# Macaron block (tree FFN, MLA attention, tree FFN): leaf-innermost w1 columns, w2 in 16 pieces, weight loads on ScalarE's queue, a table product on VectorE, and first rows of the next tree ahead

## The chip, the cores and the metric

The kernel runs on one core of a Trainium2 chip, in one launch, in fp32 (masks, positions and routing tables are bf16 where they are exact). The metric is the device time of that core in microseconds (us). The kernel before took 2531.09 us (median of 3 runs, 2529.74 to 2541.51). Engines are named as in the profile: PE is TensorE (PEld its weight loads), DVE is VectorE, ACT is ScalarE, POOL is GpSimd, SP is SyncE, which only issues DMAs. A "queue" is an engine's own list of instructions that issue DMAs: an instruction that waits there holds everything behind it on that engine.

## The reference

`x` is (4, 1024, 256), that is 4096 tokens of width 256. The block is a half-weighted FFN, an attention layer and a second half-weighted FFN with the same weights:

```python
x = x + 0.5 * ffn(layernorm(x))
x = x + attention(layernorm(x))
x = x + 0.5 * ffn(layernorm(x))

def tree(x, nw, nb, w1, b1, w2, b2, act):   # hard-routed, depth 8
    node = 0
    for _ in range(8):
        logit = x . nw[node] + nb[node]
        node = 2 * node + 1 + (logit > 0)
    leaf = node - 255                        # 256 leaves
    h = act(x @ w1[leaf] + b1[leaf])         # w1 (256, 256, 16)
    return h @ w2[leaf] + b2[leaf]           # w2 (256, 16, 256)

def ffn(x):
    xn = (x - mean) / sqrt(std + 1e-5)
    q, k, v = (tree(xn, ..., relu) for each of three trees)
    y = xn + softmax(q @ k.T / 16) @ v       # over all 1024 tokens of a row
    return y + tree(y, ..., gelu)            # the fourth tree, f
```

The attention layer has 16 heads of width 16, a latent of 128 for keys and values, rotary positions and a mask by pages of 64. The change does not touch it.

## The kernel before

**Stages.** Times are us from the span's start: FFN1 0 to 856 (routing to 117, tree q 117 to 223, tree k 232 to 328, tree v 333 to 441, softmax attention 444 to 770, tree f 770 to 856), attention layer 856 to 1690, FFN2 1690 to 2533 (routing to 1764, q 1764 to 1873, k 1874 to 1979, v 1983 to 2083, attention 2087 to 2410, then f and the output). The function `ffn` (L994) is called twice, for FFN1 with `first` set.

**Routing and sorting.** The 4096 tokens are 32 tiles of 128 in SBUF. `routes` (L421) takes the top five levels of trees q, k and v for four tiles at a time: `route` (L378) transposes the rows (L389), copies them (L392), multiplies by the nodes' weights (L397), compares (L405), and marks each token's block of 8 leaves (L409, L417); POOL adds up these marks (L419). The normalized rows also go to DRAM, `rows_x` (`keep_rows`, L372, on ACT's queue), 512 KB in each of 8 steps. Before each step `norms(k)` runs, which here also takes steps of `build` (below). `placement` (L530) then gives every token a slot, sorted by block, in blocks filled up to tiles of 128 slots: `low` computes ranks (matmuls L547, L548) and `high` the table `inv` of which token sits in which slot. In `high`, VectorE makes `tiles` (L589), ACT one half of `both` (L591), POOL the other half (L593), and PE multiplies (L596) into the table. Trees k and v are placed while the tree before them runs. `rest(3)` is the part of q's placement that remains once all tiles are routed; after its last step the first gather of tree q is issued (L806).

**A tree.** Each of q, k and v runs 48 tiles always, and up to 63 in the spare parts 48 to 53, 53 to 58, 58 to 63 under `tc.If` on the number of tiles used (`spare_leaves`, L772). In this data q and v take a spare part in one FFN or the other. `leaves` (L791) is a software pipeline over tiles: gather rows by `inv` (`load`, POOL's indirect DMA, L806, four tiles ahead, and past tile 47 too), transpose (`turn`, PE L817, ACT copy L819), multiply by the block's columns of w1, 128 columns for 8 leaves of 16 and 7 for the lower nodes (`hidden`, PE L835, L842), make the mask of the leaf that the token takes (DVE L851 to L858), mask the 128 columns (DVE L865), transpose and apply relu (`active`, PE L879, L880, ACT L888), multiply by w2 and b2 (`result`, PE L899, L900), copy out of PSUM (ACT L914, tile `og`, three buffers) and store (SP, L915). 

**Weights.** w1 arrives as (leaf, column of x, 16) in four raw parts of 1 MB (`load_part`, DMA L710, two buffers), is transposed by PE (L759) and copied to w1 by DVE (L762) and ACT (L764) in turn: `load_first` (L740) is a generator with 16 groups of four transposes and one copy, and issues raw parts 3 and 4 when 1 and 2 are used up. w2 is one 4 MB DMA to 128 partitions (`load_second`, L700), with partition (leaf, hidden column). b2 comes in three DMAs (L937), `sub` with the lower nodes in one (L744). `load_b1` (L717) makes b1 of all four trees in FFN1 by 48 small DMAs on SP (L724, L729) and POOL operations (L733 to L738). All these loads are issued from SP; ACT's queue carries `keep_rows`. While tree q runs, `with_steps` drains one step of k's placement per tile and one group of k's `load_first` per three tiles; the same with v during k. For tree q itself, `build` (the 16 groups of its `load_first`) is taken during `norms(k)` for k from 4 on, two groups each time, two more after `routes`, and the rest between the steps of `rest(3)`.

**Order.** Trees q and k and the routing are ordered by the Tile framework's scheduler; the attention and tree f are in program order (`in_order`). Completion of DMAs is counted on eight lanes shared by SP's and ACT's queues; an issue waits until its lane is free.

Of the kernel before, what the change touches and what calls it, by code (L numbers as in the profile page):

```python
# [77 lines left out]
def macaron_kernel(ctx: ExitStack, tc: tile.TileContext, a: dict, out: bass.AP):  # L78
# [107 lines left out]
    with tc.tile_pool(name="nodes", bufs=2) as np_, banks(0, 8):  # L186
        nwT = np_.tile([P, KC, len(FFFS), 2 * P], F32, name="nwT", bufs=1)
        nc.vector.memset(thr, 0.0)
        for f, nm in enumerate(FFFS):
            pt = [sm([P, 2 * P]) for _ in range(KC)]  # L190
            for lo in (0, NODES - P):
                nw = np_.tile([P, E], F32, name="nw", bufs=8)
                nc.sync.dma_start(nw, a[f"{nm}_nw"][lo : lo + P, :])
                for c in range(KC):
                    nc.tensor.transpose(
                        pt[c][:, lo : lo + P], nw[:, c * P : (c + 1) * P], ident
                    )
            lo = f % 3 * NBLK
            nc.scalar.dma_start(
                thr[lo : lo + NBLK - 1, f // 3 : f // 3 + 1],  # L200
                a[f"{nm}_nb"][: NBLK - 1].unsqueeze(1),
            )
            for c in range(KC):
                nc.vector.tensor_copy(nwT[:, c, f, :NODES], pt[c][:, :NODES])
            nc.scalar.dma_start(
                below[f].rearrange("p (c n) -> p c n", c=KC), nwT[:, :, f, NBLK - 1 : NODES]
            )
# [322 lines left out]
    def placement(pool, oh, acc, pieces, gblk, sel, own, inv, slot, ahead=False):  # L530
# [41 lines left out]
        def high(c, first, table):  # L572

            lo, hi = pieces[c]
            n, ts_ = hi - lo, slice(lo, hi)
            past, lane, in_lane = parts.pop(c)
            row = pool.tile([P, n, NBLK], F32, name="row", tag="row")
            nc.vector.tensor_tensor(row, oh[:, ts_, :], bc(first, 1, n), ALU.mult)
            at = pool.tile([P, n], F32, name="at", tag="at")
            nc.vector.tensor_reduce(at, row, AX.X, ALU.add)  # L580
            nc.vector.tensor_add(at, at, past)
            nc.vector.scalar_tensor_tensor(
                slot[:, ts_], at, float(P), lane, ALU.mult, ALU.add
            )
            yield
            tiles = pool.tile([P, n, GCOL], BF16, name="tiles", tag="tiles")
            at_b = pool.tile([P, n], BF16, name="at_b", tag="at_b")
            nc.vector.tensor_copy(at_b, at)
            nc.vector.tensor_tensor(tiles, bc(numbers, 1, n), bc(at_b, 2, GCOL), ALU.is_equal)  # L589
            both = pool.tile([P, n, 2, GCOL], BF16, name="both", tag="both", bufs=1 + ahead)  # L590
            nc.scalar.activation(both[:, :, 1], tiles, AF.Copy, scale=pid)  # L591
            yield
            nc.gpsimd.tensor_tensor(both[:, :, 0], tiles, bc(starts[:, ts_], 2, GCOL), ALU.mult)  # L593
            pi = sm([P, 2, GCOL])
            for i in range(n):
                nc.tensor.matmul(  # L596
                    pi, in_lane[:, i, :], both[:, i], start=(i == 0), stop=(i == n - 1)
                )
            yield
            if c:  # L600
                nc.vector.tensor_tensor(table, table, pi[:, 0], ALU.add)
            else:
                nc.vector.tensor_scalar_add(table, pi[:, 0], float(NTOK))
            nc.vector.tensor_tensor(table, table, pi[:, 1], ALU.add)
            yield
# [91 lines left out]
    def load_second(queue, pool, f):  # L697

        w2 = pool.tile([P, NBLK, E], F32, name=f"w2_{FFFS[f]}", tag="w2")
        dma = queue.dma_start(w2, a[f"{FFFS[f]}_w2"].rearrange("(b e) l d -> (e l) b d", e=EPB))  # L700
        if f != 3:
            tc.keep_in_program_order(dma)
        return w2
# [3 lines left out]
    def load_part(pool, f, hf, c, bufs=2):  # L707

        raw = pool.tile([P, P, LW], F32, name=f"raw_{FFFS[f]}{hf}{c}", tag="raw", bufs=bufs)
        nc.sync.dma_start(raw, a[f"{FFFS[f]}_w1"][hf * P : (hf + 1) * P, c * P : (c + 1) * P])  # L710
        return raw

    def load_raw(pool, f, bufs=2):

        return [load_part(pool, f, *p, bufs) for p in PART[:bufs]]

    def load_b1(pool, f):  # L717

        b1 = pool.tile([3 * NBLK, W1W], F32, name=f"b1_{FFFS[f]}", tag="b1", bufs=2)
        nb = a[f"{FFFS[f]}_nb"]  # L720
        nc.gpsimd.memset(b1[:, P + SUB :], 0.0)
        for k in range(3):
            at = slice(k * NBLK, (k + 1) * NBLK)
            nc.sync.dma_start(  # L724
                b1[at, :P], a[f"{FFFS[f]}_b1"].rearrange("(b e) l -> b (e l)", e=EPB)
            )
            for n in (1, 2, 4):
                lo = NBLK * n - 1
                nc.sync.dma_start(  # L729
                    b1[at, P + n - 1 : P + 2 * n - 1],  # L730
                    nb[lo : lo + NBLK * n].rearrange("(b j) -> b j", j=n),
                )
        nc.gpsimd.tensor_copy(b1p[f], b1)  # L733
# [6 lines left out]
    def load_first(pool, f, w1, raws, on_both=True, bufs=2):  # L740
# [3 lines left out]
        nc.sync.dma_start(sub, below[f].rearrange("p (c n) -> p c n", c=KC))  # L744
# [6 lines left out]
        for k, (hf, c) in enumerate(PART):  # L751
            raw = raws.pop(0)
            dst = w1[:, c, hf * nb_half : (hf + 1) * nb_half, :P].rearrange(
                "p b (e l) -> p l b e", l=LW
            )
            for l0 in range(0, LW, 4):
# [8 lines left out]
                if l0 + 4 == LW and k + 1 + len(raws) < len(PART):  # L765
                    raws.append(load_part(pool, f, *PART[k + 1 + len(raws)], bufs))
# [5 lines left out]
    def spare_leaves(*what):  # L772

        gblk = what[9]
# [9 lines left out]
        )  # L784
        with ExitStack() as es:
            for k in range(1, len(SPARE) - 1):
                es.enter_context(tc.If(used > SPARE[k], preferred_fallthrough_block=False))
                for _ in leaves(*what, k):
                    pass

    def leaves(pool, f, w1, w2, b2s, b1p, sel, own, inv, gblk, func, places, got, part=0):  # L791
# [5 lines left out]
        def load(g):  # L797
            width = E + (f == 3)
            if g < SPARE[1] + PRE:
                xg = pool.tile([P, width], F32, name="xg", tag="xg", bufs=PRE + 1 + 5 * (f // 3))  # L800
            else:
                xg = pool.tile([P, width], F32, name="xh", tag="xh", bufs=2 + 4 * (f // 3))
            if f == 3:
                nc.sync.dma_start(xg, xs_f[g * P : (g + 1) * P, :])
                return xg
            nc.gpsimd.indirect_dma_start(  # L806
                out=xg,
                out_offset=None,
                in_=rows_x,
                in_offset=bass.IndirectOffsetOnAxis(ap=inv[:, g : g + 1], axis=0),  # L810
            )
            return xg
# [8 lines left out]

        def hidden(g, xg, xT):
            if (g - lo) % REGS == 0:
                n = min(REGS, hi - g)
                _, vals = nc.values_load_multi_w_load_instructions(
                    gblk[:, g : g + n],
                    engines=[mybir.EngineType.PE],
                    min_val=0,
                    max_val=NBLK - 1,
                    skip_runtime_bounds_check_because="block numbers are limited by a minimum",  # L830
                )
                blk.update(zip(range(g, g + n), vals))
            ph = sm([P, P + SUB])
            for c in range(KC):
# [28 lines left out]
            )  # L863
            hm = pool.tile([P, P], F32, name="hm", tag="hm", bufs=3)
            nc.vector.tensor_tensor(  # L865
                hm.rearrange("p (e l) -> p e l", l=LW),
                ph[:, :P].rearrange("p (e l) -> p e l", l=LW),
                bc(mask[:, 0], 2, LW),
# [49 lines left out]
        end = hi if part else hi + PRE  # L918
        for g in range(lo - PRE, hi + 6):
            if g + PRE < end and g + PRE not in got:  # L920
# [73 lines left out]
    def ffn(first: bool, last: bool):  # L994
# [11 lines left out]
        with ExitStack() as es:  # L1006
# [25 lines left out]
            with ExitStack() as ws, banks(0, 8):  # L1032
# [5 lines left out]
                def tree(lp, f, *weights):  # L1038
                    return (
                        lp, f, *weights, b1p[f], sel[f], own[f], inv[f], gblk[f], AF.Relu, None, {}  # L1040
                    )

                with ExitStack() as hs, ExitStack() as rs:
# [11 lines left out]
                    with ExitStack() as rt:  # L1055
# [23 lines left out]
                        build = load_first(raw, 0, w1, load_raw(raw, 0))  # L1079
                        w2 = load_second(nc.sync, wp, 0)  # L1080
# [3 lines left out]
                        def norms(k):  # L1084
# [30 lines left out]
                            if k >= 4:  # L1115
                                drain(islice(build, 2))
# [3 lines left out]
                        drain(islice(build, 2))  # L1120
# [9 lines left out]
                    pp = stage(hs, "place", 1)  # L1130
                    for f in range(2):
                        what = tree(lp, f, w1, w2, b2s)
                        if first:
                            tc.keep_in_program_order(clear(nc.sync, osrt[f][SPARE[1] * P :]))
                        ahead = load_raw(raw, f + 1)
                        to = (wp, wb)[f == 0]
                        w1 = w1_of(to, f + 1)
                        w2 = load_second(nc.sync, to, f + 1)
                        b2s = load_b2(nc.sync, to, f + 1)
# [3 lines left out]
                            (3, load_first(raw, f + 1, w1, ahead)),  # L1143
                        )
                        spare_leaves(*what)
# [44 lines left out]
                what = tree(lp, 2, w1, w2, b2s)  # L1190
                with_steps(leaves(*what), (1, coming()))
                spare_leaves(*what)
# [10 lines left out]
            raws = load_raw(raw, 3)  # L1203
            with in_order(), qs, ExitStack() as ats, banks(2, 4):
                build = load_first(raw, 3, w1, raws)
# [152 lines left out]
            with banks(0, 8):  # L1358
                with in_order():
                    wp = stage(fs, "w2_f", 1, "right")  # L1360
                    w2 = load_second(nc.scalar, wp, 3)
# [13 lines left out]
                    )  # L1375
                    with_steps(leaves(*what), (1, reload()))
                spare_leaves(*what)
# [464 lines left out]
```

## Time and profile before

| what | us |
|---|---|
| median of 3 runs | 2531.09 (2529.74 to 2541.51) |
| the profiled execution's own time | 2534.66 |
| its span | 2532.9, mean granted TensorE clock 0.939 |
| PE busy | 2212.3 (87%) |
| DVE busy | 1450.0 (57%) |
| ACT busy | 1114.2 (44%) |
| POOL busy | 842.9 (33%) |

Shares of busy time are averages over stages with different limits. The profile page has the whole span in 40 slices; windows give busy time in a stretch; the timeline of one engine gives start, duration, engine, line, operation, output and inputs, count, and in square brackets the idle time of the engine just ahead of it with what ended it. A "q" behind an engine's name (SPq) marks its sequencer, which issues DMAs. A group of k instructions in a row is one line with the count at its end.

### The profile page before, as it was taken

The page shows a single profiled execution, that of the slowest core. Times are in us where ns is not written, and L with a number is a line of the kernel's source. Part 1 is how long each engine was busy: PE and PEld are TensorE (multiplying, and loading weights), DVE is VectorE, ACT ScalarE, POOL GpSimd, SP SyncE. Part 2 cuts the span into 40 slices and gives each one's busy share as a digit, 9 for nine tenths or more (in the row PEclk, how much of TensorE's full clock was granted, in tenths as well). Part 3 has the DMA queues.
Part 4 walks back from the last instruction along what each step waited for, and adds up shares of the span by engine and source line. Part 5 has one row for each costly group of instructions (what it writes and reads, how often), then busy time and mean ns, then how long its engine had stood idle before and what let it go on. Part 6 is the DMA issues. An engine that isn't in the chain of part 4 may idle for free. (4 is left out here: it accounts for less than half of the span.)

```text
span 2532.9 us, 43584 instructions
## 1 busy us (share of the span) xinstructions
PE 2212.3 (87%) x14203; PEld 1426.6 (56%) x14205; DVE 1450.0 (57%) x4720; ACT 1114.2 (44%) x2902; POOL 842.9 (33%) x1075
## 2 busy tenths in 40 slices
PE   4587988999978799999999999985979889999784
PEld 2376866666647644434344344334868766766473
DVE  6675844333446766666676677736857543334475
ACT  3354655233214225555555555552646552332142
POOL 5554565333144421101101100004545662431453
PEclk9798999999998889999999999987999899999897
DMA  9767675343065400000000000036675752430655
GB/s 320 247 196 214 173 217 154 98 126 109 22 189 150 127 1 1 1 1 1 1 18 1 1 18 12 8 136 222 174 206 165 214 158 94 134 106 23 186 158 166
DMA packets 208596, 288.03 MB, mean 114 GB/s; under 512 B 25449, under 2 KB 182522, under 8 KB 204256
## 3 DMA queue, kind: packets, MB, share of 16 engines
q1 hardware_dynamic: 133104, 156.89, 19.3%
q0 software_dynamic: 34304, 86.63, 13.0%
q10 hardware_dynamic: 40944, 41.43, 5.2%
q8 instruction: 132, 2.16, 0.4%
q14 instruction: 112, 0.92, 0.1%
HBM read 185.37 MB, written 104.32 MB: 114 GB/s over the span
## 5 line engine op out<-in xcount | busy, mean ns | idle before, releaser
L1592 DVE TENSOR_REDUCE mxh<-big 128x1 f32<-128x512 f32 (+3 forms) x768 | 392.9, 551 | 194.4 <-PE big L1584 192.5
L1628 ACT ACTIVATE pTh<-big 128x512 f32<-128x512 f32 (+3 forms) x768 | 341.3, 491 | 289.9 <-PE big L1584 266.2
L1584 PE MATMUL big<-kTh,qTh 32*128 32x512 f32 (+3 forms) x1536 | 402.2, 538 | 1.3 <-ACT kTh L1565 1.2
L1620 PE MATMUL big<-qTh,kTh 32*128 32x512 f32 (+3 forms) x1536 | 401.2, 537 | 2.1 <-ACT pTh L1628 1.8
L819 ACT COPY xgT<-sm 128x256 f32<-128x256 f32 x399 | 148.4, 373 | 288.4 <-PE sm L817 260.7
L990 PE MATMUL sm<-vb,pT 128*128 128x256 f32 x1024 | 237.2, 386 | 10.4 <-ACT pT L986 10.4
L962 PE MATMUL two<-kT,qT 128*128 128x512 f32 x512 | 236.2, 606 | 9.7 <-issue 8.2
L1620 PEld LDWEIGHTS big<-qTh,kTh 32*128 32x128 f32 x1536 | 143.4, 184 | 157.2 <-issue 126.8
L817 PE MATMUL sm<-ident,xg 128*128 128x128 f32 x792 | 162.0, 290 | 63.6 <-DMA xg<-rows_x,inv_v 17.5
L990 PEld LDWEIGHTS sm<-vb,pT 128*128 128x128 f32 x1024 | 193.1, 193 | 36.5 <-ACT pT L986 10.9
L970 DVE TENSOR_REDUCE mx<-two 128x1 f32<-128x1024 f32 x64 | 78.3, 1224 | 197.3 <-PE two L962 197.3
L851 DVE SCALAR_TENSOR_TENSOR went<-sm,sides 128x14 bf16<-128x14 f32 x399 | 67.5, 169 | 173.7 <-PE sm L842 165.6
L1639 PE MATMUL sm<-pTh,vpad 128*32 128x512 f32 (+3 forms) x1536 | 165.0, 501 | 0.0
L1584 PEld LDWEIGHTS big<-kTh,qTh 32*128 32x128 f32 x1536 | 146.2, 185 | 20.8 <-issue 14.5
L962 PEld LDWEIGHTS two<-kT,qT 128*128 128x128 f32 x512 | 94.6, 194 | 108.6 <-issue 105.0
L914 ACT COPY og<-sm 128x256 f32<-128x256 f32 x298 | 111.5, 375 | 93.3 <-DMA os_q<-og 24.6
L806 POOL DMA_INDIRECT xg<-rows_x,inv_k x104 | 104.6, 1006 | 107.0 <-PE sm L880 58.2
L806 POOL DMA_INDIRECT xg<-rows_x,inv_q x104 | 103.9, 999 | 90.6 <-PE sm L880 54.5
L817 PEld LDWEIGHTS sm<-ident,xg 128*128 128x128 f32 x792 | 86.5, 150 | 84.1 <-issue 44.5
L419 POOL TENSOR_TENSOR acc<-acc,oh 128x32 bf16<-128x32 bf16 (+1 forms) x128 | 41.3, 322 | 275.3 <-DVE oh L417 241.4
L905 POOL DMA_INDIRECT ytok<-og,tok x101 | 99.4, 984 | 82.5 <-DVE went L851 68.5
L992 DVE SCALAR_TENSOR_TENSOR xn<-sm,rs,xn 128x256 f32<-128x256 f32 x64 | 31.0, 485 | 162.2 <-PE sm L990 157.4
(364 smaller groups left out, 4697.8 us busy)
## 6 DMA issues: line engine op xcount, KB each, us to landing
xs_f<-zero ACTq DMA_DIRECT2D x14, 1028.0 KB
xg<-xs_f SPq DMA_DIRECT2D x104, 128.5 KB
os_q<-og SPq DMA_DIRECT2D x101, 128.0 KB
os_v<-og SPq DMA_DIRECT2D x101, 128.0 KB
os_k<-og SPq DMA_DIRECT2D x96, 128.0 KB
xn<-in_x SPq DMA_DIRECT2D x16, 512.0 KB
raw_q<-in_q_w SPq DMA_DIRECT2D x8, 1024.0 KB
w_q<-in_q_w SPq DMA_DIRECT2D x2, 4096.0 KB
```

The costliest lines, as they stand in the source:

```text
L806: nc.gpsimd.indirect_dma_start(out=xg, out_offset=None, in_=rows_x, in_offset=bass.IndirectOffsetOnAxis(ap=inv[:, g : g + 1], axis=0),)
L817: nc.tensor.transpose(pa[:, c, :], xg[:, c * P : (c + 1) * P], ident)
L819: nc.scalar.copy(xT, pa)
L905: nc.gpsimd.indirect_dma_start(out=places[g], out_offset=bass.IndirectOffsetOnAxis(ap=tok, axis=0), in_=og, in_offset=None, bounds_check=N ...
L914: nc.scalar.copy(og, po)
L962: nc.tensor.matmul(ps[:, n0 : n0 + 512], qT[:, c, i * P : (i + 1) * P], kT[:, c, n0 : n0 + 512], start=(c == 0), stop=(c == KC - 1),)
L990: nc.tensor.matmul(po, pT[:, j, :], vb[:, j, :], start=(j == 0), stop=(j == TPB - 1))
L1584: matmul = nc.tensor.matmul(ps[:, :n], qT[r : r + HPAD, hg, i * P : (i + 1) * P], kT[r : r + HPAD, hg, n0 : n0 + n], start=True, stop=True,)
L1592: nc.vector.tensor_reduce(maxima(b, hg)[:, i, c, u : u + 1], ps[:, :n], AX.X, ALU.max)
L1620: matmul = nc.tensor.matmul(ps[:, off:], kT[r : r + HPAD, hg, j * P : (j + 1) * P], qT[r : r + HPAD, hg, qb * QN + off : (qb + 1) * QN], s ...
L1628: nc.scalar.activation(pT[:, u, off:], ps[:, off:], AF.Exp, scale=1.0 / math.sqrt(HD))
L1639: nc.tensor.matmul(acc[r : r + HPAD, off:], vpads[b % 2][:, j, 4 * hg + 2 * pair + u, :], pTs[pair][:, u, off:], start=(j == 0), stop=(j = ...
```

## The change

- **w1's columns.** In q, k and v the 128 columns of a block are ordered with the leaf innermost, (hidden column, leaf), not (leaf, hidden column). The copies L762 and L764 write accordingly, the mask is spread over the other axis at L865, b1 is permuted by one more POOL copy, and w2's partitions follow the same order. Tree f keeps the old order.
- **w2 in 16 pieces.** With that order w2 of q, k and v is loaded by 16 DMAs of 256 KB to 8 partitions each. For k and v one piece is issued per tile of the tree before. The request to keep w2's load in program order is gone.
- **Queues.** The loads of raw w1, `sub`, w2 and b2 for k and v are issued from ACT and not from SP. Those of q and f stay on SP.
- **`build` of tree q** is no longer taken during `norms` or between `routes` and `rest`; all 16 groups are behind that point.
- **Table product.** L593 moves from POOL to VectorE, with a step of the generator between it and its matmuls; `tiles` shares a buffer with `row`.
- **First rows.** Three gathers of the next tree are issued ahead of the spare part of the tree before, into a pool of their own. The gathers past the 48 tiles are gone, and the spare parts gather for themselves. The number of used tiles is read into registers ahead of the tree.
- **nwT.** The eight copies of nodes' weights at the start (L204) move from VectorE to ACT.

```diff
@@ placement.high
-            nc.gpsimd.tensor_tensor(both[:, :, 0], tiles, bc(starts[:, ts_], 2, GCOL), ALU.mult)
+            nc.vector.tensor_tensor(both[:, :, 0], tiles, bc(starts[:, ts_], 2, GCOL), ALU.mult)
+            yield
@@ load_second
-        dma = queue.dma_start(w2, a[f"{FFFS[f]}_w2"].rearrange("(b e) l d -> (e l) b d", e=EPB))
-        if f != 3:
-            tc.keep_in_program_order(dma)
-        return w2
+        if f == 3:
+            queue.dma_start(w2, a["f_w2"].rearrange("(b e) l d -> (e l) b d", e=EPB))
+            return w2, iter(())
+        rows = a[f"{FFFS[f]}_w2"].rearrange("(b e) l d -> l e b d", e=EPB)
+
+        def pieces():
+
+            for l in range(LW):
+                queue.dma_start(w2[l * EPB : (l + 1) * EPB], rows[l])
+                yield
+
+        return w2, pieces()
@@ load_first
             dst = w1[:, c, hf * nb_half : (hf + 1) * nb_half, :P].rearrange(
-                "p b (e l) -> p l b e", l=LW
+                "p b (e l) -> p l b e" if f == 3 else "p b (l e) -> p l b e", l=LW
             )
@@ leaves.hidden
+            split = "p (e l) -> p e l" if f == 3 else "p (l e) -> p l e"
             nc.vector.tensor_tensor(
-                hm.rearrange("p (e l) -> p e l", l=LW),
-                ph[:, :P].rearrange("p (e l) -> p e l", l=LW),
-                bc(mask[:, 0], 2, LW),
+                hm.rearrange(split, l=LW),
+                ph[:, :P].rearrange(split, l=LW),
+                bc(mask[:, 0], 1 + (f == 3), LW),
                 ALU.mult,
             )
@@ leaves, the loop
-        end = hi if part else hi + PRE
         for g in range(lo - PRE, hi + 6):
-            if g + PRE < end and g + PRE not in got:
+            if g == lo - PRE:
+                numbers_of(lo)
+            if g + PRE < hi and g + PRE not in got:
                 got[g + PRE] = load(g + PRE)
@@ ffn
+                def first_rows(f):
+                    rows = [fp.tile([P, E], F32, name="xf", tag="xf", bufs=3) for _ in range(3)]
+                    return {g: gathered(xf, inv[f], g) for g, xf in enumerate(rows)}
...
-                        build = load_first(raw, 0, w1, load_raw(raw, 0))
-                        w2 = load_second(nc.sync, wp, 0)
+                        build = load_first(nc.sync, raw, 0, w1, load_raw(nc.sync, raw, 0))
+                        w2, pieces = load_second(nc.sync, wp, 0)
+                        drain(pieces)
...
-                            if k >= 4:
-                                drain(islice(build, 2))
 
                         routes(hp, (0, 1, 2), *hot, norms)
                         drain(low(2))
-                        drain(islice(build, 2))
                         if first:
                             for f in range(len(FFFS)):
                                 load_b1(b2p, f)
                         for _ in rest(3):
                             next(build, None)
                         drain(build)
...
-                        ahead = load_raw(raw, f + 1)
+                        ahead = load_raw(nc.scalar, raw, f + 1)
                         to = (wp, wb)[f == 0]
                         w1 = w1_of(to, f + 1)
-                        w2 = load_second(nc.sync, to, f + 1)
-                        b2s = load_b2(nc.sync, to, f + 1)
+                        w2, pieces = load_second(nc.scalar, to, f + 1)
+                        b2s = load_b2(nc.scalar, to, f + 1)
                         with_steps(
                             leaves(*what),
                             (1, placing(pp, f + 1)[1]()),
-                            (3, load_first(raw, f + 1, w1, ahead)),
+                            (1, pieces),
+                            (3, load_first(nc.scalar, raw, f + 1, w1, ahead)),
                         )
-                        spare_leaves(*what)
+                        got = first_rows(f + 1)
+                        spare_leaves(used, *what)
```

## The prediction

> **What bounds the kernel now.** I read the busy table and the slices first, then busy time stage by stage, then the idle time of TensorE inside the routed trees with what ended it, and last SyncE's own issue queue, because the change moves DMAs between queues. On the page:
>
> ```profile
> PE 2212.3 (87%) x14203; PEld 1426.6 (56%) x14205; DVE 1450.0 (57%) x4720; ACT 1114.2 (44%) x2902; POOL 842.9 (33%) x1075
> ...
> PE   4587988999978799999999999985979889999784
> ...
> DMA  9767675343065400000000000036675752430655
> ```
>
> TensorE is the bound nearly everywhere (87%), so work taken from any other engine counts only where TensorE waits for it. The low slices are the two routes and the trees, and there the DMA engines are busiest. The windows of FFN1's tree q, tree k, and FFN2's tree q show what is left; columns are window, length, then busy us (instructions) of PE, PEld, DVE, ACT, POOL, then granted clock, DMA share and GB/s:
>
> ```profile
> 117.00:228.00 111.00, 93.44 (x686) 80.66 (x687) 73.14 (x312) 58.65 (x180) 54.56 (x57) 0.90 0.69 201
> 228.00:329.00 101.00, 90.44 (x685) 77.54 (x685) 72.18 (x312) 58.36 (x180) 56.07 (x59) 0.95 0.71 195
> ...
> 1764.00:1873.00 109.00, 98.97 (x745) 86.05 (x743) 77.85 (x335) 63.96 (x196) 56.87 (x57) 0.94 0.59 168
> ```
>
> TensorE idles 17.6, 10.6 and 10.0 us there; ACT is idle for about 45% of each. Nothing the change does to the attention stages is on their path, so all its gain must come from such idle time in six trees, and from the routes. What ends the idle time, from TensorE's timeline (start, duration, tile, idle before and releaser):
>
> ```profile
> 134.50 0.61 PE L596 MATMUL sm<-both,in_lane 128*128 128x128 bf16 x8 [2.17 <-POOL both L593]
> ...
> 158.69 1.22 PE L899 MATMUL sm<-w_q,hid 128*128 x2 [4.30 <-ACT og L914]
> ...
> 203.06 0.70 PE L899 MATMUL sm<-w_q,hid 128*128 x2 [2.84 <-ACT hid L888]
> ...
> 230.66 0.69 PE L817 MATMUL sm<-ident,xg 128*128 128x128 f32 x2 [2.10 <-DMA xg<-rows_x,inv_k]
> ...
> 344.67 0.66 PE L817 MATMUL sm<-ident,xg 128*128 128x128 f32 x2 [5.53 <-DMA xg<-rows_x,inv_v]
> ...
> 1902.11 0.37 PE L547 MATMUL sm<-oh,tri 128*128 128x256 bf16 x1 [5.90 <-ACT og L914]
> ```
>
> The waits on og are not ACT's own slowness. SyncE's queue shows why:
>
> ```profile
> 143.31 1.33 SPq L710 DMA_DIRECT2D raw_k<-in_k_w  x1
> 144.74 24.29 SPq L915 DMA_DIRECT2D os_q<-og  x12
> ```
>
> Twelve result stores need 24.29 us there, and a 1 MB weight load stands before them on the same queue; og has three buffers, so late stores stop L914 on ACT, and with it the PSUM banks that TensorE wants.
>
> **The change, part by part.** The sum is made on the profiled execution, 2534.66 us (span 2532.9); the median of the runs is 2531.09 (2529.74 to 2541.51), so I take the same difference off the median.
>
> A. Weight loads of trees k and v leave SP's queue for ACT's. The waits behind og and hid at tile steps are 4.30, 2.84 and 1.06 in FFN1's q, 0.91, 1.00 and 0.63 in its k, 1.52, 1.53 and 2.19 in FFN2's q, 5.90 and 0.73 in its k: 22.6 us. The lower bound is 8, if the stores are slow because the DMA engines are 69% busy and not because of the queue. Twenty-four us for twelve stores is one per 2 us, about a tile's length, so I take 18: the few long waits go, some of the short ones stay.
>
> B. L593's product moves from POOL to VectorE. In the trees TensorE waits 2.17, 2.17, 2.20 and 2.25 us for it: 8.8 us. POOL takes 1.04 us (24 times); the nearest VectorE row, the same shape at L589, takes 0.68. VectorE has 28 us idle in each tree window, which hides 4 x 0.68. The step is now a separate yield ahead of the matmuls, so TensorE's wait has a tile to pass in. I take 8 (4 to 8.8). What is late next is VectorE's hm, if anything.
>
> C. Three gathers of the next tree's rows go ahead of the spare parts. The waits on xg at tree changes are 2.10 and 0.82, 1.97 and 1.83, 5.53, and 4.12: 16.4 us. The other part of a change, TensorE's idle behind the branch (4.54, 4.26, 4.93 us, put down to "issue"), stays. Four extra gathers past tile 47 (about 1 us of POOL each) go too, hidden. I take 12 (8 to 16.4), since the rows come but the first matmul still waits for the last w_k pieces and the register loads.
>
> D. FFN1's route. The built instruction order shows that SP's queue now has the 16 w_q pieces, of which the 12th on wait for the eighth write of rows_x, then b2s_q, the 48 small b1 loads, sub_q, and only then raw_q parts 3 and 4, which before went out between the b1 loads:
>
> ```profile
> 63.57 0.37 SPq L710 DMA_DIRECT2D raw_q<-in_q_w  x1
> ...
> 75.76 0.35 SPq L710 DMA_DIRECT2D raw_q<-in_q_w  x1
> ...
> 79.52 0.37 ACTq L373 DMA_DIRECT2D rows_x<-xn  x1
> ...
> 103.17 0.27 PE L547 MATMUL sm<-oh,tri 128*128 128x256 bf16 x1
> ...
> 111.18 1.08 POOL L806 DMA_INDIRECT xg<-rows_x,inv_q  x1 [2.10 <-DVE total L498]
> ```
>
> With no build inside the route I let the route's loop end some 6 us sooner, so that write lands near 79. Four pieces and b2s (7 x 0.37), then 48 loads at 0.45 (1.35 for three) take 24 us: parts 3 and 4 go out at 103. Two MB at 320 GB/s, the fastest slice of the page, take 6.6 us. A small transfer, the first gather, is in use 5 us after its issue ends (117.23); of such a start I add 2 us, as the two overlap: in at 111 to 112. The order puts L547 of the last ranks behind the 16 transposes of a part (3.37 us at 88.72): 114.5 in place of 103.17, about 11 later, and the first gather follows it by 8.0 as now. I take +10, between 2 (the raws land before the placement needs TensorE) and 18 (the small loads take 0.72 each, as three of them did at 56.17).
>
> E. FFN2's route. All 16 build groups move behind the route, which ends 5 us sooner (L405's steps were 3.7 to 4.4 apart without build groups, up to 7.7 with them). But ACT's list has pieces 5 to 14 of w_k back to back ahead of the last four w_q copies, each waiting for one of eight DMA lanes that it shares with SP. At 320 GB/s a piece of 256 KB takes 0.8 us, ten 8 us; hidden in part by the transposes. +4, from -4 to +12.
>
> F. In the trees ACT issues 64 pieces (k and v, twice) at 0.37 us: 23.7 us, one per tile of 2.3 us. No row of before shows a load to 8 partitions. From 0 (ACT's 45% idle hides them) to 24 (each delays an xgT copy); nearest is the issue of a row write on ACT at 79.52, which delayed nothing. I take +8.
>
> Nothing: the copies to w1 (L762, L764, 1.05 us with a stride; a contiguous one, L392, takes 0.59) become shorter by up to 0.46 us on engines with room; nwT's eight copies (0.42 us) change engine in the first 21 us, where loads set the pace; the masked product L865 (0.29) only reads in another order; one POOL copy per b1 ends before b1p is needed; the register load of the used tiles moves to a place ahead of the leaves, beside their own register loads. If that cover went, each would cost at most 3 us.
>
> Sum: -18 - 8 - 12 + 10 + 4 + 8 = -16: 2518.7 on the profiled time, 2515 on the median.
>
> The Trainium skill ("DMA: Bandwidth & Descriptors", section on why a DMA increments its semaphore by 16) says that the number of partitions decides how many of the 16 DMA engines serve a transfer, so a piece of 8 partitions would run on 8. No row of before can show it; by it the ten pieces of E take 16 us, E is +12 and the sum -8. The same page ("Issuing engines are not separate DMA queues") says that spreading transfers over engines saves only issue time. That speaks against A, while the row of twelve stores in 24.29 us behind raw_k speaks for it; with A at nothing the sum is +2.
>
> **The rivals.**
> 1. The routes are not delayed (parts 3 and 4 land before TensorE reaches them, POOL's accumulation frees the counts sooner). For it: no build groups in the loop. Against: the built order. D and E become 0: -38 + 8 = -30, 2501.
> 2. The stores stay slow, because the bytes and not the queue hold them. For it: DMA at 0.69 in the window. Against: the next twelve stores behind the other load. A is 0: +2, 2533.
> 3. Slower: pieces hold ACT. Each waits for a lane, and xgT, hid and og copies queue behind it, then TensorE. For it: the list of E, and 200 GB/s in the trees: a piece takes 1.3 us of the whole rate there. Against: ACT's idle 45%. Ten pieces at 2.3 us (114 GB/s, the page's mean) make E +23; F at its bound is +24; with D +10: -38 + 57 = +19, 2550. It decides from 28 us of waiting at pieces, 0.44 us for each of 64.
>
> **How the numbers follow.** Forecast 0.42, rival 1 0.16, rival 2 0.18, rival 3 0.24. 0.5%, 12.7 us, is what a measurement of this kernel can tell from no change: 2518.4 and 2543.7 bound "same". Of the forecast, whose own range is 2502 to 2530, 0.6 lies below 2518: faster 0.25 + 0.16 + 0.02 = 0.43; slower 0.22 from rival 3 and 0.04 from the others; same 0.31. The range leaves out the ends of rivals 1 and 3: 2488 to 2550.
>
> **What would show it.** A: the runs of stores in SP's queue have no load between them, and waits for og above 1 us are gone in q and k. B: no wait of L596 on POOL. C: no wait on xg after a tree change, only the 4 to 5 us of issue. D: the first gather at 121 (over 111 and under 129); raw_q parts 3 and 4 issued near 103. E: FFN2's first gather 0 to 8 us later from the route's start. F: ACT's idle time at pieces below 0.2 us each. The prediction is wrong if tree windows on TensorE shrink by under 15 us in all, if the first gather comes before 112, or if ACT stands still at a piece for more than 1 us again and again.

## The result, and the profile after

The changed kernel takes 2748.73 us (median of 4 runs, 2735.32 to 2758.43) against 2530.74 (4 runs): a ratio of 1.0847, 95% interval 1.0792 to 1.0903. That is 218 us slower, where 16 us faster was forecast and 2550 was the upper end of the range. The profiled execution has a span of 2749.8 us. The page of the changed kernel, the lines that answer to those shown of before (engines' busy time, then the slices of PE and DMA, then the DMA rate of the slices):

```profile
PE 2243.5 (82%) x14203; PEld 1448.7 (53%) x14205; DVE 1448.7 (53%) x4736; ACT 1098.1 (40%) x2911; POOL 800.0 (29%) x1039
...
PE   3247787899996979999999999950786889999874
...
DMA  8477667524315410000000000066567665241545
GB/s 244 75 198 161 164 176 213 154 90 123 104 62 176 130 63 1 1 1 1 1 17 1 1 20 13 7 149 103 157 171 125 157 199 155 80 135 42 175 136 167
```

TensorE has the same 14203 matmuls and is busy 31 us longer, at a mean granted clock of 0.905 and not 0.939; no other engine but its weight loads has more to do. The work is spread over more time. PE's slices fall to 2 and 4 in the first routing and to 5 and 0 in the second. In the second slice DMA is 0.4 busy while it moves 75 GB/s; before it was at 0.7 and 247 GB/s there.

Landmarks of the timeline (first w1 matmul of each tree, rounded to 0.1 us) give the time of each stage. x4 is the run below that takes only the pieces and the column order out:

| stage | before | after | x4 |
|---|---|---|---|
| start to tree q | 120.2 | 169.9 | 130.2 |
| q to k | 111.8 | 140.9 | 107.4 |
| k to v | 102.5 | 125.9 | 100.5 |
| v, attention, to f | 435.0 | 440.2 | 441.4 |
| f, attention layer, routing, to q of FFN2 | 996.8 | 1071.5 | 1001.2 |
| q to k | 109.5 | 115.5 | 111.3 |
| k to v | 109.3 | 143.8 | 100.2 |
| v, attention, to f | 428.1 | 422.4 | 421.4 |
| f to the end | 119.7 | 119.7 | 119.0 |
| span | 2532.9 | 2749.8 | 2532.6 |

The loss is in the two stretches with a routing (+49.7 and +74.7) and in the trees during which pieces are issued (+29.1, +23.4, +6.0, +34.5). SP's queue in the changed kernel's FFN1 (start, duration, line, output and input, count):

```profile
30.30 71.35 SPq L709 DMA_DIRECT2D w_q<-in_q_w  x16
101.77 5.36 SPq L961 DMA_DIRECT2D b2s_q<-b2i_q  x3
...
109.83 9.03 SPq L739 DMA_DIRECT2D b_q<-in_q_nb  x3
...
143.65 0.85 SPq L719 DMA_DIRECT2D raw_q<-in_q_w  x2
```

The 16 pieces hold the queue for 71 us, 4.5 us each on average; b2s_q and the small b1 loads follow, and raw parts 3 and 4 leave at 143.65, not at 103. TensorE's timeline of the changed kernel, with its idle time and releaser in brackets:

```profile
148.89 1.94 PE L773 MATMUL sm<-ident,raw_q 128*128 128x128 f32 x8 [51.30 <-DMA raw_q<-in_q_w]
...
209.97 1.22 PE L922 MATMUL sm<-w_q,hid 128*128 x2 [8.37 <-ACT hid L911]
...
1926.45 1.95 PE L773 MATMUL sm<-ident,raw_q 128*128 128x128 f32 x8 [83.00 <-DMA raw_q<-in_q_w]
```

Two waits for raw_q, 134 us together, cover the 124 us by which the two stretches with a routing grew. In FFN2 SP's queue is again what raw_q waits for:

```profile
1793.17 75.56 SPq L709 DMA_DIRECT2D w_q<-in_q_w  x16
1873.37 32.76 SPq L961 DMA_DIRECT2D b2s_q<-b2i_q  x3
...
1911.54 0.83 SPq L719 DMA_DIRECT2D raw_q<-in_q_w  x2
```

ACT's timeline of the same kernel shows the wait inside a tree, and pieces that hold ACT:

```profile
209.09 0.37 ACT L937 COPY og<-sm 128x256 f32<-128x256 f32 x1 [10.49 <-DMA os_q<-og]
...
1852.72 44.80 ACTq L709 DMA_DIRECT2D w_k<-in_k_w  x11
```

In a tree, result stores wait among the pieces, og's three buffers run out, and ACT stands for 10.49 us ahead of xgT and hid; TensorE's 8.37 at 209.97 is that wait. In FFN2's routing eleven pieces of w_k hold ACT for 44.80 us, in front of the last copies of w_q. That ends at 1897.5, though, and those copies need raw_q, which TensorE gets at 1926.45: the late raw parts on SP set the time there, not ACT.

### The profile page after: what moved, and what is told of

Its sections match the earlier page's. It is cut to its first block, busy times and chain, and to the rows that moved or that the text cites. A ratio compares the mean times of both kernels' runs of the same rounds, so it can differ in the third digit from the quotient of the medians.

```text
span 2749.8 us, 43596 instructions
## 1 busy us (share of the span) xinstructions
PE 2243.5 (82%) x14203; PEld 1448.7 (53%) x14205; DVE 1448.7 (53%) x4736; ACT 1098.1 (40%) x2911; POOL 800.0 (29%) x1039
## 5 line engine op out<-in xcount | busy, mean ns | idle before, releaser
L773 PE MATMUL sm<-ident,raw_q 128*128 128x128 f32 x128 | 24.0, 360 | 134.3 <-DMA raw_q<-in_q_w 134.3
L810 POOL DMA_INDIRECT xg<-rows_x,inv_k x90 | 89.4, 994 | 140.5 <-PE sm L835 77.2
L888 DVE TENSOR_TENSOR hm<-sm,mask 128x128 f32<-128x128 f32 x399 | 115.4, 289 | 11.1
```

The costliest lines, as they stand in the source:

```text
L810: nc.gpsimd.indirect_dma_start(out=xg, out_offset=None, in_=rows_x, in_offset=bass.IndirectOffsetOnAxis(ap=inv[:, g : g + 1], axis=0),)
L888: nc.vector.tensor_tensor(hm.rearrange(split, l=LW), ph[:, :P].rearrange(split, l=LW), bc(mask[:, 0], 1 + (f == 3), LW), ALU.mult,)
```

## The experiments

Each kernel is the changed one or the one before with the edit shown. Before took 2616 to 2617 us on the chips of x6 to x14 and 2528 to 2534 on the others, so ratios are to before on the same chip, and stages are compared only on one kind of chip. x2 to x5, x10 and x15 were executed once each. In the expectations P is the theory that neighbouring partitions make a piece slow, N that half of the DMA engines do, and O that the order of SP's queue does.

### What a piece costs: x2, x3, x4, x10

**x4**: no column order, no pieces; everything else of the change stays.

```diff
-            for l in range(LW):
-                queue.dma_start(w2[l * EPB : (l + 1) * EPB], rows[l])
-                yield
+            queue.dma_start(w2, a[f"{FFFS[f]}_w2"].rearrange("(b e) l d -> (e l) b d", e=EPB))
+            yield
... (the column order of before, in `load_first`, b1 and `hidden`)
```

> The changed kernel with the old column order and w2 as one DMA of 4 MB to 128 partitions, on the queue and at the place of the first piece; all other parts of the change stay. P and N: 2510-2550 (what the prediction made of the change without its price for pieces: 2507 to 2523 at its central terms, and the raw parts late by some 10 us). O: 2700-2750. Against x2 it tells what 8 or 16 issues cost against 1.

**x3**: the old column order, and 16 pieces to 8 partitions that lie 16 apart.

```diff
-                queue.dma_start(w2[l * EPB : (l + 1) * EPB], rows[l])
+                queue.dma_start(w2.rearrange("(e l) b d -> l e b d", l=LW)[l], rows[l])
... (the column order of before, as in x4)
```

> The changed kernel with the old column order (leaf, hidden column) and w2 in 16 pieces as before of 256 KB and 8 partitions, which now lie 16 apart. P: the packets take 46-60 ns again, w2_q is issued in under 35 us, total 2530-2600. N: still 8 engines, so the pieces are as slow as in the changed kernel and the time stays at 2720-2760. O: 2700-2750.

**x2**: the new column order, 8 pieces to 16 partitions that lie 8 apart.

```diff
-            for l in range(LW):
-                queue.dma_start(w2[l * EPB : (l + 1) * EPB], rows[l])
+            for e in range(EPB):
+                queue.dma_start(w2.rearrange("(l e) b d -> e l b d", e=EPB)[e], rows[:, e])
```

> The changed kernel with w2 of q, k and v in 8 pieces of 512 KB, one for each leaf place, to 16 partitions that lie 8 apart (the column order is kept). Theory P (the 8 neighbouring partitions of a piece are what limits it: in the changed kernel 1 KB packets of pieces take 150 ns and not 46, and a piece moves at 58 GB/s): w2_q is issued in under 30 us and not 71, and the time falls to 2520-2580. Theory N (only half of the DMA engines serve a piece): the same here, 2520-2580, since 16 partitions bring all engines. Theory O (the order of SP's queue, raw parts 3 and 4 behind w2, b2 and the small b1 loads, whatever a piece costs): 2700-2750.

**x10**: as x4, with 16 pieces to all 128 partitions.

```diff
+            every = a[f"{FFFS[f]}_w2"].rearrange("(b e) l d -> (e l) b d", e=EPB)
             for l in range(LW):
-                queue.dma_start(w2[l * EPB : (l + 1) * EPB], rows[l])
+                two_ = slice(l * NBLK // LW, (l + 1) * NBLK // LW)
+                queue.dma_start(w2[:, two_], every[:, two_])
... (the column order of before, as in x4)
```

> Like x4 (old column order, all else as changed), but w2 of q, k and v in 16 pieces of 256 KB again, each to all 128 partitions (two of the 32 blocks a piece). Theory: what a piece costs is where it lands (how many partitions, and how near each other), not that there are 16 issues and 16 lanes taken; then w2_q is issued in under 25 us and the total is within 15 us of x4's 2534. Rival (number of issues and lanes): as x3, 2600 and more.

| kernel | w2 of a tree goes in | time, us | before, same chip | w2_q's issue, us |
|---|---|---|---|---|
| changed | 16 to 8 neighbouring partitions | 2748.73 | 2530.74 | 71.35 |
| x3 | 16 to 8 partitions 16 apart | 2646.49 | 2527.57 | 58.37 |
| x2 | 8 to 16 partitions 8 apart | 2548.57 | 2527.57 | 40.97 |
| x10 | 16 to 128 partitions | 2642.28 | 2616.11 | 22.03 |
| x4 | 1 to 128 partitions | 2534.37 | 2527.57 | 0.38 |

x4 stands at 1.0027 where the changed kernel stands at 1.0847, and x2, which keeps the new column order, at 1.0083: the pieces are the loss. Windows in which little but such loads moves show why; columns are as in the windows of before, and the last three are granted clock, share of the 16 DMA engines and GB/s. The changed kernel, then x3, x2 (with some of the writes of rows_x) and x4 (w_q to 128 partitions, with some of b2i and rows_x):

```profile
96.00:104.00 8.00, 1.60 (x8) 1.27 (x6) 4.63 (x12) 1.99 (x3) 0.00 (x0) 0.71 0.57 58
```

```profile
84.00:90.00 6.00, 2.82 (x14) 2.75 (x14) 3.88 (x16) 1.06 (x1) 2.58 (x8) 0.78 0.56 106
```

```profile
72.00:78.00 6.00, 3.71 (x17) 1.52 (x15) 4.88 (x17) 4.22 (x9) 2.12 (x4) 1.00 1.06 210
```

```profile
49.00:52.00 3.00, 2.33 (x9) 1.32 (x9) 0.65 (x4) 2.58 (x8) 2.54 (x4) 0.50 1.09 377
```

A share above 1 says that these shares come out some per cent too high; 0.57 and 0.56 are half of 1.09. So pieces to 8 partitions run on half of the engines, in x3 as well, and x2's run on all. But a busy engine (16 times the share) does not move the same in each: 58 / 9.1 = 6.4 GB/s with 8 neighbouring partitions, 106 / 9.0 = 11.8 with 8 that lie 16 apart, 210 / 17.0 = 12.4 with 16 that lie 8 apart, and 377 / 17.4 = 21.6 with 128. So neither theory P (neighbours) nor N (half of the engines) is enough: x3 was to land at 2530 to 2600 by P and at 2720 to 2760 by N, and landed at 2646; and w2_q's issue, which P put under 35 us in x3 and under 30 in x2, took 58.37 and 40.97. Half of the engines, times half the rate for few partitions, times half again for neighbours make 58 of 377 GB/s.

So 6.4 GB/s is what one such piece got out of an engine, not an engine's limit: in FFN2's routing of the changed kernel pieces of w_q (SP) and of w_k (ACT) were in flight together, and the same share of the engines moved nearly twice as much, half of it from each queue:

```profile
1853.00:1866.00 13.00, 0.00 (x0) 0.00 (x0) 0.00 (x0) 0.00 (x0) 0.00 (x0) 0.50 0.56 105
```

From the changed kernel to x3 only the partitions differ. From x3 to x2 and x4 the source differs too (1 KB out of every 16 KB of w2 in x3, 16 KB out of every 128 in x2, all of it in x4), and no run changes the source alone.

Theory O fell with x4, and the number of issues with x10, whose pieces go out in 22 us:

```profile
29.16 22.03 SPq L711 DMA_DIRECT2D w_q<-in_q_w  x16
```

x10 stands at 1.010 of before, though, in its one execution, where x4 stands at 1.0027 and its repeat x18 at 1.0033. Some 17 to 19 us may belong to 16 issues, more than the 15 that its theory allowed; the executions of before on that chip lie between 2604 and 2627 us, so this stays open.

### The order of the routing: x5, x6

**x5** is the changed kernel, **x6** is x4, both with

```diff
+                            if k >= 4:
+                                drain(islice(build, 2))
...
                         drain(low(2))
+                        drain(islice(build, 2))
```

> The changed kernel with tree q's build groups taken inside the routing again, as before (two in each step from the fifth on, two after the routing); pieces as changed. O: raw parts 3 and 4 are asked for early, the first gather of tree q comes back to 111-125 us and the time falls by 80-130. P and N: the raw parts are still behind 71 us of w2 pieces on SP's queue, so the routing waits inside its loop and the time stays within 40 us of 2749.

> x4 (old column order, w2 in one DMA, all other parts of the change) with tree q's build groups taken inside the routings again. Theory (terms D and E of the prediction are right: x4's first w_q matmul came 10.0 us later than before's, and FFN2's routing took 4.4 more): both go, so 10 to 14 us less than x4, whose one run stood at 1.0027 of before: 0.997 to 0.999. Rival (the groups cost the routing loop as much as they save behind it): 1.002 to 1.004.

x5 stands at 1.0855 of before, the changed kernel at 1.0847, so the order alone does nothing while pieces stand ahead on the queue. SP's queue in x5:

```profile
29.95 70.58 SPq L709 DMA_DIRECT2D w_q<-in_q_w  x16
...
108.47 11.48 SPq L719 DMA_DIRECT2D raw_q<-in_q_w  x2
```

The raw parts go out 35 us sooner than in the changed kernel, and tree q begins at 172.2 all the same, not 169.9. x6 missed: 1.0036 (1.0007 to 1.0065). Tree q begins at 125.0, against 124.4 in x14 on the same chip, which has the old order too; x4's began 10.0 us after before's. So the routing's 10 us come back. But tree q then takes 114.7 us, and x14 103.7 on the same chip. ACT's timeline of x6 and then TensorE's show most of the 11 us:

```profile
131.71 6.28 ACTq L757 DMA_DIRECT2D sub_v<-below_v  x1
```

```profile
138.52 1.27 PE L856 MATMUL sm<-w_q,xgT 128*128 x4 [6.19 <-ACT xgT L836]
...
209.62 0.16 PE L502 MATMUL sm<-upto,tri 32*32 32x1 bf16 x1 [2.35 <-DVE total L498]
```

ACT waits 6.28 us to issue sub_v behind 4 MB of w_k. x4 has the same wait (5.88), x14 2.20.

### The three gains, one at a time: x7, x8, x9, x12, x13, x14, x15, x16, x17, x18

**x7** (A): the kernel before with the loads of k and v on ACT.

```diff
-                        w2 = load_second(nc.sync, to, f + 1)
-                        b2s = load_b2(nc.sync, to, f + 1)
+                        w2 = load_second(nc.scalar, to, f + 1)
+                        b2s = load_b2(nc.scalar, to, f + 1)
```

(raw parts and sub likewise)

> The kernel before with term A alone: raw w1, sub, w2 (one DMA) and b2 of k and v issued from ACT, nothing else changed. As predicted: -18 (-8 to -22.6), so 0.991 to 0.997 of before. Rival (what leaves SP's queue comes back on ACT's: an issue waits there for one of the lanes that both queues share and holds xgT, hid and og behind it, as sub_v did for 5.9 us in x4): within 5 us of before, 0.998 to 1.002.

**x8** and **x17** (B): L593 on VectorE and its yield, as in the diff of the change.

> The kernel before with term B alone: L593's product on VectorE and the extra step. As predicted: -8 (-4 to -8.8) in the four tree waits, and a little in the routing; 0.996 to 0.999. Rival (VectorE, 70% busy in trees, delays went and hm by as much): 1.000 or above.

> x8 again (L593 on VectorE, nothing else) with more rounds, since its interval reached 1.0001. As x8: 0.996 to 0.999. If it is 1.000 or above, B is worth nothing and x8 was chance.

**x9** (C): `first_rows` of the change, the gathers past a part's end gone, `tiles` in `row`'s buffer.

> The kernel before with term C alone: three first rows of the next tree ahead of the spare parts, no gathers past a part's end, one buffer shared to make room for it. As predicted: -12 (-8 to -16), 0.994 to 0.997. Rival (the wait for rows at a change of trees moves to the fourth row or to the first matmul behind the register loads, and a spare part that is taken starts without rows): 0.999 to 1.003.

**x12**: A, B and C. **x14**: x12 with `b2s = load_b2(...)` a line ahead of `w2 = load_second(...)`. **x16**: x14 without C. **x13**: B, raw parts alone on ACT, b2 ahead of w2 on SP.

> The kernel before with terms A, B and C (weights of k and v on ACT with w2 in one DMA, L593 on VectorE, three first rows of the next tree ahead, no gathers past a part), and with neither the new column order nor the build moved out of the routing. The prediction's terms: -38, so 0.985. What x4 showed outside the routings, stage by stage: -15, so 0.993 to 0.996 (2512 to 2520). If it is not below 0.998, the three terms were worth nothing together.

> x12 (A, B and C) with the three b2 DMAs issued ahead of w2 on ACT. Theory (x12 lost what it won by ACT standing at b2s_v behind the 4 MB of w_v for 11.9 and 12.3 us at the changes from q to k): some 22 us less than x12, 0.998 to 1.000, and no wait over 3 us of L835 on xgT at those changes. Rival (whatever follows the 4 MB waits there): 1.004 to 1.009.

> The kernel before with terms A and B and b2 issued ahead of w2, without C. Theory (C costs about 0.4% by itself, x9, and x14 with A, B and C stood at 1.0003): 0.994 to 0.998, the fastest of all. Rival (A gains nothing even so, and x14's zero is not made of a gain and a loss): 0.998 to 1.001, B alone.

> The kernel before with term B, and of A only what the trace of x7 paid for: the raw parts of k and v on ACT; sub, b2 and w2 stay on SP, b2 ahead of w2 so that it does not wait for a lane behind 4 MB. In x7 the tiles of q and k in both FFNs took 6, 0, 3 and 8 us less than in x8 on the same chip, 17 in all, and the two tree changes 11.8 and 10.6 more, in which ACT stood at b2s_v. Theory: B's 0.998 and the 17 us: 0.990 to 0.994. Rival (it is w2 and b2 on SP, not the raw parts, that hold the stores): 0.997 to 0.999.

**x18** is x4 again, timed; **x15** is the kernel before, unchanged.

> x4 again (the whole change but the column order and the pieces), timed, since x4 was one look. From x4: 1.0027. From the terms measured alone on other chips (A 1.0021, B 0.9977, C 1.0041, the build behind the routing +10 and +4.4 us): 1.004 to 1.010. If it is below 0.998, the rest of the change is a gain and the prediction was wrong in the pieces alone.

> The kernel before, unchanged, for a profile on the same chip as the three beside it, so that terms A, B and C can be put down stage by stage. All theories: the time of before. If the stage that differs between the first profile of before and this one is tree v, tree f and the attention (as in the runs of x7 and x8), then the chips differ there and terms have to be read as ratios; if it is the same as the first profile, the table needs no care.

| kernel | what | ratio to before (95%) |
|---|---|---|
| x7 | A | 1.0021 (1.0002 to 1.0040) |
| x8 | B | 0.9977 (0.9953 to 1.0001) |
| x17 | B, other chip | 0.9949 (0.9931 to 0.9967) |
| x9 | C | 1.0041 (1.0017 to 1.0065) |
| x12 | A, B, C | 1.0073 (1.0048 to 1.0099) |
| x14 | A, B, C, b2 first | 1.0003 (0.9981 to 1.0026) |
| x13 | B, raw parts on ACT, b2 first | 1.0002 (0.9973 to 1.0031) |
| x16 | A, B, b2 first | 0.9935 (0.9917 to 0.9953) |
| x18 | all but pieces and column order | 1.0033 (1.0016 to 1.0049) |

x15 took 2536.29 us beside 2534.3 for before, and its stages are within 5 us of the first profile's; x16 to x18 ran on that chip.

x12 missed: with A, B and C it was to be at 0.993 to 0.996. So did x13, which was to be at 0.990 to 0.994.

A's mechanism is there and is paid back. From first to last w1 matmul, the 48 tiles of q and k in FFN1 and of q and k in FFN2 take 87.5, 87.7, 102.0 and 86.9 us in x7, and 93.5, 90.5, 102.3 and 94.8 in x8 on the same chip: 17 us less, as forecast for A (18). But ACT's timeline of x7 at the change from q to k says where they went:

```profile
219.57 0.39 ACTq L700 DMA_DIRECT2D w_v<-in_v_w  x1
220.05 12.40 ACTq L937 DMA_DIRECT2D b2s_v<-b2i_v  x3
232.55 0.65 ACT L819 COPY xgT<-sm 128x256 f32<-128x256 f32 x2 [16.15 <-issue]
```

b2s_v waits behind the 4 MB of w_v, now on the engine that makes xgT: TensorE waits 11.76 us there and 10.61 in FFN2. In before the same issue took 11.98 us on SP, where it held no engine that computes. With b2 ahead of w2 (x14 for x12) 0.7% comes back, 18 us, and the long wait is gone. Even so A is worth little: x16 and x17 ran side by side at 0.9935 and 0.9949, with intervals that overlap. x13's raw parts on ACT, with 1.0002, won nothing over B alone.

C is a loss by itself. The waits on rows at the tree changes are gone from x9, but TensorE's timeline of x9 shows what came (in FFN1's v and FFN2's q, at the start of the spare part that is taken):

```profile
447.65 1.27 PE L832 MATMUL sm<-w_v,xgT 128*128 x4 [2.71 <-ACT xgT L816]
...
1903.71 0.73 PE L832 MATMUL sm<-w_q,xgT 128*128 x4 [3.40 <-ACT xgT L816]
...
2027.15 0.80 PE L814 MATMUL sm<-ident,xf 128*128 128x128 f32 x4 [4.67 <-issue]
```

The spare part starts without rows, since the gathers past tile 47 were given up, and the 4.67 us of "issue" at a tree change stay. The two waits on xgT are 6 us of the 11 by which x9 is slower; where the other 5 are is open.

x16 beats both kernels: 2517.43 us against 2534.3 for before on its chip.

## Why the prediction was wrong, point by point

- **What failed is the price of a piece.** Part E had "at 320 GB/s a piece of 256 KB takes 0.8 us, ten 8 us"; part D counted w_q's last pieces at their issue (0.37 us); part F bounded a piece by its issue alone (24 us for all). The rate of a full-width load was taken for one to 8 partitions. Measured: 4.5 us a piece, 71 us for a tree's w2. The term F (+8) stands for +93 in the four trees q and k (29.1 + 23.4 + 6.0 + 34.5), gains of A to C included; D (+10) for +49.7; E (+4) for most of +74.7, where w_q's pieces and b2s_q held SP for 108 us.
- **Half of the engines.** The Trainium skill ("DMA: Bandwidth & Descriptors", section on why a DMA increments its semaphore by 16) has the number of engines right: 8 by its rule, and a share of 0.57 in the window above where a load to all partitions shows 1.09. The 16 us for ten pieces that the prediction worked out from it were too few by 2.8 times, since what a busy engine moved fell from 21.6 to 6.4 GB/s too.
- **Rival 3 had a right mechanism, but not the main one.** Pieces hold ACT: all 64 took about 100 us there, of which 24 are the issue by part F's 0.37 us, so some 75 us were waiting, where 28 were to decide. Nearly half of the 100, 44.80 us for eleven pieces, lies in FFN2's routing, where ACT was not what TensorE waited for. The rival was given +19. It left out the main part, SP: raw parts 3 and 4 behind w_q's own pieces, 51.30 and 83.00 us.
- **D was right without the pieces, E by luck.** In x4 tree q begins 10.0 us later than before (forecast 10), the first gather starts at 123.94 (forecast 121), and raw parts went out at 98.08 and 105.06 (forecast 103). FFN2's stretch with the routing grows by 4.4, where E had 4; but E was made up of pieces on ACT, which x4 doesn't have, and of a routing that ends 5 us sooner.
- **A** was right in its tiles (17 for 18) and wrong in its sum. The prediction named the lanes that both queues share, for the pieces, and priced no wait on them for the small loads behind 4 MB at the tree changes (22 us in x7).
- **B** was right in kind and too small on one chip: 13 us at 0.9949, 6 at 0.9977, forecast 8. The four waits of over 2 us for L593 in the trees are gone in all kernels with it.
- **C** had the wrong sign: -12 forecast, +11 measured. It priced the rows won at the tree changes and left out the rows lost at the spare parts.
- In sum, the change without pieces was forecast at -24 or so (A to C less D and E) and is +8 (1.0033): so even with the price right the forecast would have missed the side.

## What to carry to other kernels

Before a tile is loaded in slices of partitions, work out its rate from how many partitions a slice has and how near they lie, not from the bytes: here 16 slices of 8 neighbouring partitions moved at 58 GB/s where the full tile moved at 377. A layout that needs such a load costs it again on every queue behind it, so ask what stands next in that queue, and put small loads ahead of large ones where an engine that computes also issues. A prefetch that is paid for by giving up another has to be costed at both ends.

## What the runs showed of the hardware that was not expected

- What a busy DMA engine moves depends on the partitions of the transfer: 21.6 GB/s with 128 partitions, 12.4 with 16 that lie 8 apart, 11.8 with 8 that lie 16 apart, 6.4 with 8 neighbours, nearly all in runs of 1 KB. Two pieces to 8 neighbours each, in flight together, moved 105 GB/s at the share of the engines at which one moved 58.
- Eight partitions showed 0.56 to 0.57 of the 16 engines busy, neighbours or not, where 16 partitions showed 1.06 and 128 showed 1.09: half of the engines against all.
- The same program took 2616 to 2617 us on two of the chips and 2528 to 2534 on the others, 3.4% apart. In x7 and x8 the time lies in tree v, tree f and the attention, with PE idle for 0.9 to 1.1 us at every other tile of tree v, which the profile puts down to "issue".
